# An RWKV block: a chunk's first columns set beside the product of k and v, the channel mix's gate through the hyperbolic tangent, and a new table of turns

## The chip, the cores and the metric

The kernel runs on one core of a Trainium2 chip. The engines of that core have short names in the profile: PE is TensorE (matmul; PEld is its weight load), DVE is VectorE, ACT is ScalarE, POOL is GpSimd and SP is SyncE, which here only issues transfers (DMA). The metric is device time in microseconds (us), the median of several runs; less is better.

## The reference, cut to what matters

The block takes x of shape 8 x 256 x 512 (batch, token, channel) in 32-bit floats and a state per batch. The 512 channels are 32 heads of 16.

```python
xn = _ln(x, ln1_w, ln1_b)
sx = _token_shift(xn, state[:, i1])                 # previous token minus this one
xxx = jnp.tanh((xn + sx * maa_x) @ maa_w1).reshape(b, l, 5, 1, EXTRA_MAA)
xxx = jnp.matmul(xxx, maa_w2).reshape(b, l, 5, E)
x5 = xn[:, :, None] + sx[:, :, None] * (maa_stack + xxx)
w = jnp.exp(-jnp.exp(time_decay + jnp.tanh(x5[:, :, 1] @ decay_w1) @ decay_w2))
r, k, v = x5[:, :, 3] @ Wr.T, x5[:, :, 0] @ Wk.T, x5[:, :, 2] @ Wv.T
g = jax.nn.silu(x5[:, :, 4] @ Wg.T)
def step(s, rkvw):                                  # one token after another
    a = k_t[:, :, :, None] * v_t[:, :, None, :]
    out = jnp.einsum('bhk,bhkd->bhd', r_t, u * a + s)
    return (a + w_t[:, :, :, None] * s, out)
...                                                 # att: group norm over the 16 values of a head
x = x + att * g @ Wo.T
xn2 = _ln(x, ln2_w, ln2_b)
sx2 = _token_shift(xn2, state[:, i0])
xk = xn2 + sx2 * ffn_maa_k
xr = xn2 + sx2 * ffn_maa_r
rr = jax.nn.sigmoid(xr @ ffn_Wr.T)                  # the gate of the channel mix
kk = jnp.square(jax.nn.relu(xk @ ffn_Wk.T))
x = x + rr * (kk @ ffn_Wv.T)
```

## The kernel before, in words

The code does not issue instructions as it goes along. A `Plan` first records each piece of work as an `Op` with its engine, the buffers that it writes and reads, and a function that issues it. Then `Plan.order` strings the pieces together as a list scheduler. It takes them by rank, lets a piece claim a buffer of a pool when one is free, and so fixes the order of the instructions on every engine and which buffer each piece gets. The rank comes from a table of numbers, `TURNS`, that has 25 rows: one for the setup, then for each of the eight batches one for `inputs_of_scan`, one for `scan` and one for `rest`. The planner's own costs of work and transfers (`LANDS`, `SWITCH` and others) decide where two pieces compete. After that each engine runs its list in order, and a piece waits on semaphores for what it needs.

`inputs_of_scan(b)` makes, for the 256 tokens of batch b, the layer norm (`xh`, `xn`), the token shift `sx`, the small product with a hyperbolic tangent (`psx`, `ta`), the five mixed inputs (`psm`, `mix`), the projections to k, v, r and g, and the decay w. `rest(b)` does the group norm, the output projection Wo, the second layer norm and the channel mix (Wfk, Wfr, Wfv), whose weights are streamed anew for each batch into buffers `Ws`. The helper `mul` (L401) issues the matmuls of all projections. Some of them are split into four of 32 columns.

`scan(b)` is the recurrence over tokens. It is split into 4 blocks of 4 chunks per batch, 128 chunks in all. A chunk holds 4 value columns of all heads: 128 partitions by 4 times 256 tokens. It passes these steps, with the line numbers before the change:

- A transfer by SP copies v, from memory, over the partitions into `vs` (128x1024). There are six buffers `vs`.
- L911, on ACT: the first column of each of the four stretches of 256 is overwritten with the state at the start (from `s0`, `cm`), 4 numbers per partition.
- L918, on DVE (6 of 128 chunks: L915, on POOL): the whole of `vs` is multiplied by k shifted by a token. The DVE reads k from a copy `kp` in PSUM, POOL reads the buffer of k itself. Column 0 of that k is set to one, so the first columns pass unchanged.
- L920, on DVE: the scan over the 1024 positions writes `st`, with `wrep` holding w, or zero at a stretch's first position. `wrep` is made by ACT in L901, once per block; there is one such buffer.
- L923, on POOL: `st` is multiplied by r.
- L931, on PE: after four chunks the gather of the block sums over the keys of a head into `pat`; L937, on DVE, adds it to `att`.

The channel mix has three gate lines: L1026 (ACT, Sigmoid from PSUM into `o`), L1051 and in the last batch L1044 (DVE, `o` times the product `psfv`). L1017 and L1018 (ACT) are Relu and Square of `kk`. ACT needs a table of functions for exp, tanh and the others. Where the next function is of another set, a table load (L1086) is put in front. Tanh was counted to the set of exp.

Other lines that are spoken of: L516 copies the centered weights Wv from PSUM (ACT), L534 makes four head masks `hm` (DVE), L613 transposes `xh`, L714 makes `ta` by Tanh (ACT), L743, L745 and L755 belong to the mixes of the first batch, L818 makes the decay (ACT), L856 the gate `g` by Silu, L997 and L1002 the group norm's end (`att` on ACT, `att` times `g` on POOL), L1008 adds x to the output projection (DVE).

Of the kernel before, what the change touches and what calls it, by code (L numbers as in the profile page):

```python
# [9 lines left out]
AF = mybir.ActivationFunctionType  # L10
ALU = mybir.AluOpType
# [47 lines left out]
class Op:  # L59
    def __init__(self, engine, us, outs, ins, emit, mode):  # L60
        self.engine, self.us, self.emit, self.mode, self.narrow = engine, us, emit, mode, False
        self.bufs = list(dict.fromkeys([*outs, *ins]))
        self.before, self.after, self.waits = [], [], 0
        self.ready = self.start = self.end = 0.0
        self.number, self.kind = 0, engine + "".join(c for c in self.bufs[0].name if not c.isdigit())


class Plan:
# [5 lines left out]
    LANDS = {"vs__": (2.3, 1.8), "rsb_": (0.9, 2.0), "sq_": (0.9, 2.0), "s": (0.2, 1.9), "vo_": (0.75, 2.2), "vo__": (0.38, 2.2), "o_": (0.75, 1.1), "x": (1.6, 1.7), "xt": (1.6, 1.7), "xs": (0.7, 0.9), "idt": (0.2, 2.2), "rd": (0.4, 1.4)}  # L74
    SWITCH = {"ACT": 1.3, "PE": 0.12}
    TABLES = {"exp": "exp_and_others", "silu": "silu_and_others", "sig": "sigmoid_and_others", "sqrt": "sqrt_and_others"}
# [15 lines left out]
    def add(self, engine, us, outs, ins, emit, mode=None, into=(), lag=0.0, kb=0, part=False):  # L92
# [3 lines left out]
        if kb:  # L96
            op.wire, op.lag = self.LANDS.get("".join(c for c in op.bufs[0].name if not c.isdigit()), (kb / 327, 2.3))

# [17 lines left out]
    def stage(self):  # L116
# [1045 lines left out]
```

## Time and profile before

| what | value |
| --- | --- |
| median of 3 runs | 609.05 us (608.36 to 609.75) |
| the profiled execution's own time | 609.75 us |
| its span in the profile | 607.9 us |
| granted TensorE clock | 1.00 throughout |
| PE busy | 598.3 us, 98% |
| DVE, ACT, POOL busy | 543.6, 514.6, 520.0 us |
| memory traffic | 124.76 MB, 205 GB/s on average |

The span runs from the first to the last instruction on the core. The time of the execution has 1.85 us more. PE is nearly always busy, but a share of busy time is an average: in the stretch from about 34 to 155 us POOL too is busy without a pause, and the last 28 us have hardly any work but matmuls. Weights and x are read in 512 KB transfers, the broadcasts of `vs` are 128 transfers of the same size.

### The profile page before, as it was taken

What the parts mean: (1) busy time and instruction counts of PE and PEld (TensorE: products, weight loads), DVE (VectorE), ACT (ScalarE), POOL (GpSimd) and SP (SyncE); (2) the same over time, 40 slices, a digit from 0 to 9 for tenths busy, and PEclk for the clock granted to TensorE, in tenths of its full rate; (3) what the DMA queues carried; (4) which work ended last, traced back from release to release, by engine and by line L of the source; (5) the groups of instructions that cost most, each with busy time, mean ns of one, the idle gap of its engine ahead of it and who ended that gap; (6) DMA issues with size and microseconds to landing.
All of it is one profiled execution on the core that took longest, in us unless ns stands there. A gap on an engine that the chain in (4) does not pass through costs nothing.

```text
span 607.9 us, 17606 instructions
## 1 busy us (share of the span) xinstructions
PE 598.3 (98%) x7270; PEld 346.1 (57%) x7270; DVE 543.6 (89%) x492; ACT 514.6 (85%) x1172; POOL 520.0 (86%) x417
## 2 busy tenths in 40 slices
PE   9999999999999999999999999999999999999997
PEld 7675555467544664377553775465644464547464
DVE  6699999999999998899889999999999999995442
ACT  5878779999999999998999898999989799966350
POOL 2899999999899999899988988999898998898020
PEclk9999999999999999999999999999999999999999
DMA  9889954878878887859677896788669877951552
GB/s 324 226 242 236 226 149 143 226 179 217 220 218 217 214 223 196 221 149 264 179 211 189 268 234 192 201 242 217 182 167 279 203 195 224 268 174 46 181 172 93
DMA packets 52639, 124.76 MB, mean 205 GB/s; under 512 B 5840, under 2 KB 11344, under 8 KB 52560
## 3 DMA queue, kind: packets, MB, share of 16 engines
q1 hardware_dynamic: 48048, 119.39, 71.4%
q10 hardware_dynamic: 4512, 4.26, 2.2%
q8 instruction: 57, 0.93, 0.7%
q14 instruction: 22, 0.18, 0.1%
HBM read 115.25 MB, written 8.39 MB: 203 GB/s over the span
## 4 chain that ended last, share of the span: by engine, by line
PE 72%; POOL 14%; ACT 4%; DVE 4%; issue 3%; DMA 1%; DVEq 0%; POOLq 0%; ACTq 0%
PE ps L401 59%; PE ps L931 7%; POOL st L923 7%; DVE st L920 2%; POOL mix L755 2%; PE ps L613 2%; POOL vs L915 2%; PE ps L795 2%; DMA vs<-vo 1%; ACT L1086 1%; PE ps L524 1%; POOL mix L783 1%; DVE vs L918 1%; POOL sx L641 1%; POOL att L887 1%
## 5 line engine op out<-in xcount | busy, mean ns | idle before, releaser
L920 DVE TENSOR_TENSOR_SCAN st<-wrep,vs 128x1024 f32<-128x1024 f32 x128 | 288.2, 2276 | 3.9 <-ACT wrep L901 1.8
L923 POOL TENSOR_TENSOR st<-st,r 128x1024 f32<-128x1024 f32 x128 | 254.5, 2006 | 9.4 <-DVE st L920 9.0
L918 DVE TENSOR_TENSOR vs<-vs,ps 128x1024 f32<-128x1024 f32 x122 | 143.7, 1207 | 4.2 <-ACT vs L911 4.0
L401 PE MATMUL ps<-Ws,mix 128*32 128x512 f32 (+3 forms) x872 | 115.8, 586 | 0.0
L401 PEld LDWEIGHTS ps<-Ws,mix 128*32 128x32 f32 (+1 forms) x872 | 38.4, 116 | 62.4 <-issue 55.6
L755 POOL TENSOR_TENSOR mix<-mix,xn 128x512 f32<-128x512 f32 x62 | 66.6, 1096 | 6.9 <-DVE mix L739 5.5
L931 PE MATMUL ps<-st,con 128*32 128x256 f32 x1024 | 62.1, 380 | 0.8 <-POOL st L923 0.7
L401 PE MATMUL ps<-mix,Wv 128*32 128x256 f32 (+1 forms) x832 | 60.5, 380 | 1.6 <-DVE mix L752 0.9
L401 PE MATMUL ps<-mix,Wk 128*32 128x256 f32 (+1 forms) x952 | 59.2, 379 | 0.1
L401 PE MATMUL ps<-mix,Wg 128*32 128x256 f32 (+1 forms) x664 | 58.8, 379 | 0.0
L401 PE MATMUL ps<-mix,Wr 128*32 128x256 f32 (+1 forms) x688 | 58.5, 380 | 0.0
L401 PE MATMUL ps<-mix,Ws 128*32 128x256 f32 (+1 forms) x664 | 57.7, 379 | 0.2 <-ACT mix L1017 0.2
L401 PE MATMUL ps<-Ws,g 128*32 128x512 f32 (+1 forms) x416 | 56.9, 593 | 0.2 <-POOL g L1002 0.2
L1086 ACT ACT_TABLE_LOAD x42 | 53.9, 1283 | 0.7
L737 ACT ACTIVATE ps<-ps,vec 128x256 f32<-128x256 f32 x112 | 47.6, 445 | 3.8 <-PE ps L401 2.3
L881 ACT COPY att<-ps 32x256 f32<-32x256 f32 x128 | 46.6, 364 | 4.4 <-ACT v L826 1.3
L669 POOL TENSOR_TENSOR mix<-mix,xn 128x512 f32<-128x512 f32 x44 | 47.3, 1093 | 3.4 <-ACT mix L667 3.3
L401 PEld LDWEIGHTS ps<-mix,Wv 128*32 128x32 f32 (+1 forms) x832 | 37.6, 116 | 21.3 <-DVE mix L752 1.6
L401 PEld LDWEIGHTS ps<-mix,Ws 128*32 128x32 f32 (+1 forms) x664 | 40.2, 124 | 15.8 <-ACT mix L1017 0.6
L401 PEld LDWEIGHTS ps<-mix,Wr 128*32 128x32 f32 (+1 forms) x688 | 39.3, 123 | 16.5 <-issue 1.3
L401 PEld LDWEIGHTS ps<-mix,Wg 128*32 128x32 f32 (+1 forms) x664 | 39.9, 124 | 14.8 <-issue 0.7
L931 PEld LDWEIGHTS ps<-st,con 128*32 128x32 f32 x1024 | 32.7, 110 | 27.5 <-issue 4.3
(134 smaller groups left out, 951.7 us busy)
## 6 DMA issues: line engine op xcount, KB each, us to landing
vs<-vo SPq DMA_DIRECT2D x128, 512.0 KB, 5.7
Ws<-in_fk SPq DMA_DIRECT2D x16, 512.0 KB, 5.8
Ws<-in_wo SPq DMA_DIRECT2D x16, 512.0 KB, 5.9
Ws<-in_fr SPq DMA_DIRECT2D x16, 512.0 KB, 6.1
Ws<-in_fv SPq DMA_DIRECT2D x16, 512.0 KB, 5.6
x<-in_x SPq DMA_DIRECT2D x9, 512.0 KB, 7.6
vo<-v ACTq DMA_DIRECT2D x15, 256.0 KB, 5.3
out<-o SPq DMA_DIRECT2D x15, 256.0 KB, 4.5
```

Source lines behind the costliest of these rows:

```text
L401: nc.tensor.matmul(out[i : i + n], lhsT=w[:, i : i + n], rhs=x, start=first, stop=final)
L613: nc.tensor.transpose(to[:, m, n * P : (n + 1) * P], xh[n]()[:, k * P : (k + 1) * P], idt())
L669: gp(512, t, [t, xn[q]], lambda q=q, t=t: nc.gpsimd.tensor_tensor(t(), t(), xn[q]()[:, :, 1 : T + 1], ALU.add))
L737: act(256, p_, [p_, vec], lambda g=g, q=q, m=m, p_=p_: nc.scalar.activation(p_()[:, m, :], p_()[:, m, :], AF.Identity, bias=col(f"maa_{g}" ...
L755: gp(512, t, [t, xn[q]], lambda q=q, t=t: nc.gpsimd.tensor_tensor(t(), t(), xn[q]()[:, :, 1 : T + 1], ALU.add))
L795: nc.tensor.matmul(pd()[i : i + 32, 0, :], lhsT=w, rhs=src[k // 2]()[:, k % 2, :], start=(k == begin), stop=(k == end))
L881: act(350, atts[q], [pc], lambda i=32 * (2 * q + m), m=m, q=q, h=32 * h: nc.scalar.copy(atts[q]()[h : h + 32, m, :], pc()[i : i + 32, 0, :]))
L918: dve(4 * T, [vs], [vs, kp], lambda m=m, vs=vs, kp=kp: nc.vector.tensor_tensor(vs(), vs(), kp()[:, m : m + 1, :].to_broadcast([P, 4, T]), ...
L920: dve(4 * T, [st], [w, vs], lambda w=w, vs=vs, st=st: nc.vector.tensor_tensor_scan(st().rearrange("p n t -> p (n t)"), w().rearrange("p n ...
L923: gp(4 * T, st, [st, r], lambda m=m, st=st, r=r: nc.gpsimd.tensor_tensor(st(), st(), r()[:, m : m + 1, :].to_broadcast([P, 4, T]), ALU.mul ...
L931: nc.tensor.matmul(pat()[32 * i : 32 * i + 32, 0, :], lhsT=con()[:, s : s + 32], rhs=done[i]()[:, j, :], start=(j == 0), stop=(j == 3),)
L1086: nc.scalar.preload_act_table_set(plan.TABLES[table])
```

## The change

Three edits in the code, and a new table.

**First columns.** The DMA of a chunk now writes `vs` under a second name, `landed`, and the ACT instruction that sets the first columns depends on `landed` and writes a third name, `first`. The product works on columns 1 to 255 of each stretch alone (128x4x255 in place of 128x1024), and only the scan needs `first`. So in the plan the product no longer follows the first columns. In the built program most of the DVE products waited on ACT before; now only some 15 of 122 do, and the scans wait on ACT.

**Gate.** Sigmoid becomes Tanh of half the argument, and the product becomes (`o` + 1) times `psfv` in one instruction with two operations. The missing factor of one half is put into Relu as a scale of 0.5**0.5 ahead of the Square. Tanh is counted to either the set of exp or that of silu, whichever is loaded. The program has 37 table loads with the one at its start, in place of 43. Up to the load for the square roots of batch 0's group norm it has 8 in place of 7.

**Turns and costs.** `TURNS` is another table, and some of the planner's costs are others. The number of pieces on each engine is unchanged: PE 400, DVE 490, ACT 1102, POOL 405, transfers 251. Of these PE has 185 in another place, mostly by one place and at most nine, DVE 341, ACT 968, POOL 293, transfers 211.

```diff
-    LANDS = {"vs__": (2.3, 1.8), "rsb_": (0.9, 2.0), ...}
+    LANDS = {"vs__": (2.3, 1.45), "rsb_": (0.5, 0.5), ...}
+    WAY = 1.4
+    TABLES = {"exp": "exp_and_others", "tanh": "exp_and_others", "silu": "silu_and_others", ...}
...
     TURNS = """
-        1 69 8 22 53 86 91 104 59 88 92 103 194 171 11 27 85 123 124 180 9 7 10 38 39 63 31 52 68 37 41 44 46 47 48,
+        8 74 18 43 53 81 61 64 90 79 102 99 173 150 5 33 118 145 151 146 24 15 34 26 47 49 31 46 56 30 35 48 32
...
+            if op.engine == "ACT":
+                if want == "tanh" and now in ("exp", "silu"):
+                    want = now
+                elif now == "tanh" and want in ("exp", "silu"):
+                    mode["ACT"] = now = want
...
-                    b.slot = max((s for s in self.pools[b.pool] if s[0] <= at), key=lambda s: s[0])
+                    b.slot = max((s for s in self.pools[b.pool] if s[0] + ahead <= at), key=lambda s: s[0])
...
+    def tables(self, ops):
+        mode = "sqrt"
+        for n, op in enumerate(ops):
+            want = op.mode
+            if want == "tanh":
+                want = mode if mode in ("exp", "silu") else next((o.mode for o in ops[n:] if o.mode != "tanh"), "exp")
+                want = "silu" if want == "silu" else "exp"
+            if want != mode:
+                op.table, mode = self.TABLES[want], want
...
+                landed, first = plan.fixed(vs, "landed"), plan.fixed(vs, f"vs{b}_{blk}_{i}")
...
-                act(4, vs, [s0, cm], lambda i=i, blk=blk, vs=vs: nc.scalar.activation(
+                plan.add("ACT", 0.19336, [first], [s0, cm, landed], lambda i=i, blk=blk, vs=vs: nc.scalar.activation(
                     vs()[:, :, 0:1], s0()[:, blk, 4 * i : 4 * i + 4].rearrange("p (n o) -> p n o", o=1),
-                    AF.Identity, bias=cm()[:, blk : blk + 1]), pointers=1)
+                    AF.Identity, bias=cm()[:, blk : blk + 1]), into=[vs])
...
-                        vs(), vs(), k.place[:, m : m + 1, 1 : T + 1].to_broadcast([P, 4, T]), ALU.mult), 1.815)
+                        vs()[:, :, 1:T], vs()[:, :, 1:T], k.place[:, m : m + 1, 2 : T + 1].to_broadcast([P, 4, T - 1]), ALU.mult), 1.95)
...
-                        vs(), vs(), kp()[:, m : m + 1, :].to_broadcast([P, 4, T]), ALU.mult))
-                dve(4 * T, [st], [w, vs], lambda w=w, vs=vs, st=st: nc.vector.tensor_tensor_scan(
+                        vs()[:, :, 1:T], vs()[:, :, 1:T], kp()[:, m : m + 1, 1:T].to_broadcast([P, 4, T - 1]), ALU.mult))
+                dve(4 * T, [st], [w, vs, first], lambda w=w, vs=vs, st=st: nc.vector.tensor_tensor_scan(
...
-            act(512, t, [ps], lambda t=t, ps=ps: nc.scalar.activation(t(), ps(), AF.Relu))
+            act(512, t, [ps], lambda t=t, ps=ps: nc.scalar.activation(t(), ps(), AF.Relu, scale=0.5**0.5))
...
-                o(), ps().rearrange("p m t -> p (m t)"), AF.Sigmoid), "sig")
+                o(), ps().rearrange("p m t -> p (m t)"), AF.Tanh, scale=0.5), "tanh")
...
-            dve(512, [o], [o, ps], lambda o=o, ps=ps: nc.vector.tensor_tensor(
-                o(), o(), ps().rearrange("p m t -> p (m t)"), ALU.mult))
+            dve(512, [o], [o, ps], lambda o=o, ps=ps: nc.vector.scalar_tensor_tensor(
+                o(), o(), 1.0, ps().rearrange("p m t -> p (m t)"), ALU.add, ALU.mult), 1.28)
```

What the table does is seen in the order of the instructions. Three places matter below. A row there reads line, operation, output<-inputs, shape and count; the number behind a name is the buffer's. Line numbers of the changed code are about 31 higher, so L401 is L432 there and L911 is L944.

The first place is the DVE at the head of the program, some 15 to 22 us into it: the mixes of the first batch (`mix`, L749, L752) and the head masks `hm`. Before:

```order
L749 SCALAR_TENSOR_TENSOR ps_172<-ps_172,vec,sx_104 128x256 x2
L752 TENSOR_TENSOR mix_115<-ps_172,xn_100 128x512
L534 TENSOR_SCALAR hm<-con,vec 128x32
L861 TENSOR_REDUCE cm_85<-s_83 128x4
L749 SCALAR_TENSOR_TENSOR mix_112<-ps_171,vec,sx_103 128x256
L749 SCALAR_TENSOR_TENSOR mix_114<-wrep_169,vec,sx_104 128x256 x2
L534 TENSOR_SCALAR hm<-con,vec 128x32 x2
L749 SCALAR_TENSOR_TENSOR mix_110<-ps_175,vec,sx_103 128x256 x2
```

And after the change, the same place:

```order
L780 SCALAR_TENSOR_TENSOR ps_175<-ps_175,vec,sx_104 128x256 x2
L783 TENSOR_TENSOR mix_115<-ps_175,xn_100 128x512
L780 SCALAR_TENSOR_TENSOR mix_110<-ps_172,vec,sx_103 128x256
L780 SCALAR_TENSOR_TENSOR mix_114<-wrep_169,vec,sx_104 128x256
L780 SCALAR_TENSOR_TENSOR mix_112<-ps_173,vec,sx_103 128x256
L780 SCALAR_TENSOR_TENSOR mix_114<-wrep_169,vec,sx_104 128x256
L780 SCALAR_TENSOR_TENSOR mix_110<-ps_172,vec,sx_103 128x256
L565 TENSOR_SCALAR hm<-con,vec 128x32
```

The masks have moved behind the products that POOL's next instructions read (`mix_114`, `mix_110`).

The second place is the same engine at the first chunks, some 28 to 36 us into the program. Before:

```order
L781 SCALAR_TENSOR_TENSOR mix_113<-ps_175,vec,sx_103 128x256
L918 TENSOR_TENSOR vs_145<-vs_145,ps_172 128x1024
L534 TENSOR_SCALAR hm<-con,vec 128x32
L920 SCALAR_TENSOR_TENSOR st_153<-wrep_169,vs_145 128x1024
L918 TENSOR_TENSOR vs_146<-vs_146,ps_172 128x1024
L920 SCALAR_TENSOR_TENSOR st_154<-wrep_169,vs_146 128x1024
```

After:

```order
L812 SCALAR_TENSOR_TENSOR mix_108<-ps_170,vec,sx_104 128x256
L951 TENSOR_TENSOR vs_145<-vs_145,ps_172 128x4x255
L953 SCALAR_TENSOR_TENSOR st_153<-wrep_169,vs_145 128x1024
L951 TENSOR_TENSOR vs_146<-vs_146,ps_172 128x4x255
L953 SCALAR_TENSOR_TENSOR st_154<-wrep_169,vs_146 128x1024
```

The last mask no longer stands between the first product and the first scan.

The third place is ACT at the decay and the gate of batch 1, some 80 to 93 us into the program, while batch 0 is in its scan's last blocks. `w` is the decay (L818), `g` the gate (L856), `vs` the first columns (L911). Before:

```order
L737 ACTIVATE ps_173<-ps_173,vec 128x256 x2
L1086 ACT_TABLE_LOAD
L856 ACTIVATE g_137<-ps_175 128x512
L1086 ACT_TABLE_LOAD
L818 ACTIVATE w_132<-ps_173,vec 128x256 x2
...
L826 COPY r_128<-ps_175 128x2x256
L1086 ACT_TABLE_LOAD
L856 ACTIVATE g_138<-ps_173 128x512
```

After:

```order
L1117 ACT_TABLE_LOAD
L887 ACTIVATE g_137<-ps_173 128x512
L944 ACTIVATE vs_148<-s_83,cm_85 128x4
L1117 ACT_TABLE_LOAD
L849 ACTIVATE w_132<-ps_174,vec 128x256
L944 ACTIVATE vs_147<-s_82,cm_84 128x4
L849 ACTIVATE w_133<-ps_172,vec 128x256
L849 ACTIVATE w_132<-ps_174,vec 128x256
L930 COPY ps_171<-k_125 128x512
L1117 ACT_TABLE_LOAD
L887 ACTIVATE g_138<-ps_173 128x512
L944 ACTIVATE vs_149<-s_83,cm_85 128x4
```

The second gate, `g_138`, now comes ahead of the last piece of the decay, and a further table load follows it. On PE the four matmuls of this decay stand ahead of batch 0's third gather; before they stood behind it.

More of the change, by code (lines that the diff above doesn't have):

```diff
@@ L61, in __init__ @@
         self.engine, self.us, self.emit, self.mode, self.narrow = engine, us, emit, mode, False
+        self.table = None
         self.bufs = list(dict.fromkeys([*outs, *ins]))
@@ L73 @@
     LATENCY = {"PE": 0.24, "DVE": 0.14, "ACT": 0.14, "POOL": 0.1, "DMA": 1.65}
-    LANDS = {"vs__": (2.3, 1.8), "rsb_": (0.9, 2.0), "sq_": (0.9, 2.0), "s": (0.2, 1.9), "vo_": (0.75, 2.2), "vo__": (0.38, 2.2), "o_": (0.75, 1.1), "x": (1.6, 1.7), "xt": (1.6, 1.7), "xs": (0.7, 0.9), "idt": (0.2, 2.2), "rd": (0.4, 1.4)}
+    LANDS = {"vs__": (2.3, 1.45), "rsb_": (0.5, 0.5), "sq_": (0.5, 0.5), "s": (0.3, 1.4), "vo_": (0.7, 1.4), "vo__": (0.35, 1.4),
+             "o_": (0.7, 1.2), "x": (1.8, 1.3), "xt": (1.7, 1.3), "xs": (0.7, 0.9), "idt": (0.2, 1.6)}
+    WAY = 1.4
+    TABLES = {"exp": "exp_and_others", "tanh": "exp_and_others", "silu": "silu_and_others", "sig": "sigmoid_and_others",
+              "sqrt": "sqrt_and_others"}
     SWITCH = {"ACT": 1.3, "PE": 0.12}
-    TABLES = {"exp": "exp_and_others", "silu": "silu_and_others", "sig": "sigmoid_and_others", "sqrt": "sqrt_and_others"}
     AHEAD = {"PE": 0.2}
@@ L96, in add @@
         if kb:
-            op.wire, op.lag = self.LANDS.get("".join(c for c in op.bufs[0].name if not c.isdigit()), (kb / 327, 2.3))
+            op.wire, op.lag = self.LANDS.get("".join(c for c in op.bufs[0].name if not c.isdigit()), (kb / 308, 1.7))
         op.bufs += [b for b in into if b not in op.bufs]
@@ L263, in order @@
         free = dict.fromkeys(self.LATENCY, 0.0)
-        mode, done, queue, put_off, wire, lanes = dict.fromkeys(free), [], [], [], 0.0, [0.0] * 8
+        mode, done, queue, put_off, wire, lanes = dict.fromkeys(free), [], [], [], [], [0.0] * 8
+        mode["ACT"] = "sqrt"
         for n, op in enumerate(self.ops):
@@ L303, in order @@
             if op.wire:
-                landed = max(wire if op.engine == "DMA" else 0.0, op.start + 1.2) + op.wire
-                wire = landed if op.engine == "DMA" else wire
+                landed = max([l for s, l in wire[-16:] if s <= op.start] + [op.start + self.WAY]) + op.wire
+                wire.append((op.start, landed))
                 lanes.append(landed + 1)
@@ L326, in order @@
         self.tiles([op for op in done if op.engine == "PE"])
+        self.tables([op for op in done if op.engine == "ACT" and op.mode])
         return done
+    def tables(self, ops):
[7 more added lines that the diff above has]
+                op.table, mode = self.TABLES[want], want
     def tiles(self, ops):
@@ L386, in new, with dma @@
         return Buf(pool, name, VIEWS.get(pool, lambda t: t))
-    def dma(out, in_, dst, kb, src=None, lag=0.0, part=False):
-        plan.add("DMA", 0.6, [out] if out else [], [src] if src else [], lambda: nc.sync.dma_start(out=dst(), in_=in_()),
+    def dma(out, in_, dst, kb, src=None, lag=0.0, part=False, also=()):
+        plan.add("DMA", 0.6, [out, *also] if out else [], [src] if src else [], lambda: nc.sync.dma_start(out=dst(), in_=in_()),
                  lag=lag, kb=kb, part=part)
@@ L533, in head_masks @@
         for k in range(NK):
-            dve(32, [hm], [con, vec], lambda k=k: nc.vector.tensor_scalar(
+            dve(76, [hm], [con, vec], lambda k=k: nc.vector.tensor_scalar(
                 hm()[:, k, :], con()[:, C_HM : C_HM + 32], col("faaaa", k), None, ALU.mult))
@@ L583, in normed @@
                     dve(512, [t], [s, mv, rs], lambda n=n, t=t, s=s: nc.vector.tensor_scalar(
[L584 removed]
+                        t(), s(), mv()[:, n, 0:1], rs()[:, n : n + 1], ALU.subtract, ALU.mult), 0.775)
                     xh.append(t)
@@ L627, in turned @@
                     dve(256, [xn], [ps, vec], lambda m=m, k=k, xn=xn, ps=ps: nc.vector.tensor_scalar(
-                        xn()[:, m, 1 : T + 1], ps()[:, m, :], col("ln1_w", k), col("ln1_b", k), ALU.mult, ALU.add))
+                        xn()[:, m, 1 : T + 1], ps()[:, m, :], col("ln1_w", k), col("ln1_b", k), ALU.mult, ALU.add), 1.5)
                     t = ps
@@ L633, in turned @@
                     dve(256, [xn], [ps, vec], lambda m=m, k=k, xn=xn, ps=ps: nc.vector.tensor_scalar(
-                        xn()[:, m, 1 : T + 1], ps()[:, m, :], col(f"ln{which}_w", k), col(f"ln{which}_b", k), ALU.mult, ALU.add))
+                        xn()[:, m, 1 : T + 1], ps()[:, m, :], col(f"ln{which}_w", k), col(f"ln{which}_b", k), ALU.mult, ALU.add), 1.5)
                 else:
@@ L713, in inputs_of_scan @@
             pe(0.432 * len(ks), [px], [w1, *dict.fromkeys(xin[k // 2] for k in ks)], mm, into=[ta])
-        act(256, ta, [px], lambda: nc.scalar.activation(ta(), px()[:, 0, :], AF.Tanh), "exp")
+        act(256, ta, [px], lambda: nc.scalar.activation(ta(), px()[:, 0, :], AF.Tanh), "tanh")
         def mixed():
@@ L800, in inputs_of_scan @@
         for rows in (slice(0, 64), slice(64, 128)):
-            act(T, hd, [pd], lambda rows=rows: nc.scalar.activation(hd()[rows, 1, :], pd()[0:64, 0, :], AF.Tanh), "exp")
+            act(345, hd, [pd], lambda rows=rows: nc.scalar.activation(hd()[rows, 1, :], pd()[0:64, 0, :], AF.Tanh), "tanh")
         for rows in (slice(0, 64), slice(64, 128)):
-            act(T, tb, [pd], lambda rows=rows: nc.scalar.activation(tb()[rows, :], pd()[64:128, 0, :], AF.Tanh), "exp")
+            act(345, tb, [pd], lambda rows=rows: nc.scalar.activation(tb()[rows, :], pd()[64:128, 0, :], AF.Tanh), "tanh")
         ws = [hd, new("w", f"w{b}_1")]
@@ L1043, in rest @@
                     pe(1.72 * wide / T, [ps], [*kk, *Wfv], mm, into=[y])
-                    dve(wide, [y], [o, ps], lambda yy=yy, o=o, ps=ps, cols=cols, wide=wide: nc.vector.tensor_tensor(
-                        yy()[:, cols], o()[:, cols], ps()[:, 0, 0:wide], ALU.mult))
+                    dve(wide, [y], [o, ps], lambda yy=yy, o=o, ps=ps, cols=cols, wide=wide: nc.vector.scalar_tensor_tensor(
+                        yy()[:, cols], o()[:, cols], 1.0, ps()[:, 0, 0:wide], ALU.add, ALU.mult), 1.28)
                     dve(wide, [y], [y, t], lambda yy=yy, t=t, cols=cols: nc.vector.tensor_tensor(
@@ L1079, in tile_rwkv_block @@
             phases[b + i].append((i, plan.stage()))
-    table = "sqrt"
     with tc.manual_schedule():
@@ L1083, in tile_rwkv_block @@
             narrow = op.narrow
-            if op.engine == "ACT" and op.mode and op.mode != table:
-                table = op.mode
-                nc.scalar.preload_act_table_set(plan.TABLES[table])
+            if op.table:
+                nc.scalar.preload_act_table_set(op.table)
             op.emit()
```

6 lines of the change are left out of this document (3 added, 3 removed), and 245 rows, old and new, of the table TURNS.

## The prediction

> **What bounds the kernel now.** I read the page first: the busy shares and the chain that ended last.
>
> ```profile
> PE 598.3 (98%) x7270; PEld 346.1 (57%) x7270; DVE 543.6 (89%) x492; ACT 514.6 (85%) x1172; POOL 520.0 (86%) x417
> PE 72%; POOL 14%; ACT 4%; DVE 4%; issue 3%; DMA 1%; DVEq 0%; POOLq 0%; ACTq 0%
> ```
>
> The change removes no matmul, so with PE at 598.3 us of a span of 607.9 all that can be won without making an instruction faster is PE's idle time, 9.6 us. Where that lies, and what fills it, a table of windows tells. Its columns are the window, its length, the busy time of PE, PEld, DVE, ACT and POOL with their instructions, the granted clock, the DMA share and GB/s.
>
> ```profile
> 0.00:34.30 34.30, 31.87 (x283) 24.81 (x284) 22.92 (x50) 25.73 (x61) 21.15 (x37) 1.00 0.82 260
> 34.30:155.40 121.10, 118.83 (x1734) 72.95 (x1731) 119.76 (x96) 105.70 (x246) 120.64 (x86) 1.00 0.79 206
> 155.40:312.00 156.60, 155.67 (x1969) 86.18 (x1968) 146.91 (x120) 148.32 (x343) 145.47 (x115) 1.00 0.77 208
> 312.00:580.00 268.00, 267.20 (x3207) 146.68 (x3200) 245.61 (x212) 226.26 (x510) 228.55 (x177) 1.00 0.74 206
> 580.00:608.00 28.00, 24.70 (x92) 15.45 (x89) 8.40 (x18) 8.62 (x15) 4.23 (x4) 1.00 0.34 113
> ```
>
> From 34.3 to 155.4 POOL has 120.64 us of work in 121.10. The list of its waits there has one line, and the timeline shows what ends the stretch: the multiplication by r of batch 1's last chunk (of its fourth block), and the gather that needs it.
>
> ```profile
> POOL st L923 <- DVE st L920: 0.2, 1, 0.2
> 153.33 2.02 POOL L923 TENSOR_TENSOR st<-st,r 128x1024 f32<-128x1024 f32 x1
> 155.49 1.93 PE L931 MATMUL ps<-st,con 128*32 128x256 f32 x32
> ```
>
> So POOL's work sets that this gather starts at 155.5. The 2.27 us in which PE is idle in this stretch are no gain by themselves: PE would reach the gather sooner and wait there. From 155.4 on PE is the bound, idle for 0.93 and 0.80 us in two windows, then 3.30 us in the last, most of it behind the last matmul. Its waits from 155.4 to the end are these:
>
> ```profile
> PE ps L401 <- DVE o L1051: 0.8, 1, 0.8
> PE ps L613 <- DVE xh L583: 0.4, 1, 0.4
> PE ps L401 <- ACT mix L1017: 0.2, 1, 0.2
> PE ps L401 <- DVE att L937: 0.2, 1, 0.2
> ```
>
> They add to 1.6 us. A gain has three places: POOL's start at 34.3, the length of POOL's stretch, and these waits.
>
> **First columns.** The groups that the chunk is made of (busy us and mean ns, then the idle time ahead of them and its releasers):
>
> ```profile
> L920 DVE TENSOR_TENSOR_SCAN st<-wrep,vs 128x1024 f32<-128x1024 f32 x128 | 288.2, 2276 | 3.9 <-ACT wrep L901 1.8 <-PE ps L931 0.9
> L918 DVE TENSOR_TENSOR vs<-vs,ps 128x1024 f32<-128x1024 f32 x122 | 143.7, 1207 | 4.2 <-ACT vs L911 4.0
> L911 ACT ACTIVATE vs<-s,cm 128x4 f32<-128x4 f32 x128 | 36.8, 299 | 4.5 <-DMA vs<-vo 3.3 <-ACT v L826 0.4
> L923 POOL TENSOR_TENSOR st<-st,r 128x1024 f32<-128x1024 f32 x128 | 254.5, 2006 | 9.4 <-DVE st L920 9.0
> ```
>
> The edit lets the product start without L911. What it can free is the 4.0 us that DVE waits for L911. The instruction of ACT stays (128 of 299 ns), and the scan, right behind the product on the same engine, waits for it instead. A product takes 1.2 us and a first column 0.3, so most of these waits are covered by the product from now on. But DVE is not the bound: the scan and the product make 1.207 + 2.276 = 3.48 us per chunk, yet in the stretch the end is set by POOL, which waited only 0.2 us for a scan, and after 155.4 by PE. Of the 4.0 us, 1.19 lie ahead of the very first product:
>
> ```profile
> 30.30 1.22 DVE L918 TENSOR_TENSOR vs<-vs,ps 128x1024 f32<-128x1024 f32 x1 [1.19 <-ACT vs L911]
> 31.44 0.58 DVE L534 TENSOR_SCALAR hm<-con,vec 128x32 f32<-128x32 f32 x1
> 31.94 2.28 DVE L920 TENSOR_TENSOR_SCAN st<-wrep,vs 128x1024 f32<-128x1024 f32 x1
> 34.30 2.00 POOL L923 TENSOR_TENSOR st<-st,r 128x1024 f32<-128x1024 f32 x1 [0.21 <-DVE st L920]
> 30.16 1.02 ACT L901 ACTIVATE wrep<-w 128x1020 f32<-128x1020 f32 x1
> ```
>
> There the scan also loses the mask between it and the product (0.50 us), and could start when `wrep` ends, at 31.18. POOL's wait began at 34.30 − 0.21 = 34.09; before that it was busy, so no more than the 0.21 us of its wait is won unless POOL's earlier work comes sooner.
>
> The product covers 1020 of 1024 elements: 4/1024 of 1207 ns is 5 ns, nothing. Its rows now start on the second word of each stretch. A row for such starts exists: the tile of L1008 is written from an odd word in one half of its instructions and from an even word in the other. The six products on POOL stand beside it.
>
> ```profile
> L1008 DVE TENSOR_TENSOR x<-ps,x x16: 667/684/694, 122.8 to 575.5; 128x512 f32<-128x512 f32 x16
> L915 POOL TENSOR_TENSOR vs<-vs,k x6: 2007/2202/2407, 40.2 to 123.9; 128x1024 f32<-128x1024 f32 x6
> ```
>
> L1008 spreads by 4% in all, and by no more between the halves, so I cost the odd start on DVE at nothing. On POOL three products take about 2.01 us and three about 2.4, by the block's place in k. The new addresses of k and `vs` differ, and which of the two prices the six take the trace can't say: 6 x (2.01 − 2.20) = −1.2 to 6 x (2.41 − 2.20) = +1.2 us, on the path, since POOL is without a pause. I take 0, the middle, and keep both ends.
>
> **The gate.**
>
> ```profile
> L1051 DVE TENSOR_TENSOR o<-o,ps 128x512 f32<-128x512 f32 x15 | 10.1, 678 | 17.6 <-PE ps L401 17.5
> L1044 DVE TENSOR_TENSOR o<-o,ps 128x256 f32<-128x256 f32 x1 | 0.4, 420 | 0.3 <-PE ps L401 0.3
> L662 DVE SCALAR_TENSOR_TENSOR mix<-sx,vec,xn 128x256 f32<-128x256 f32 x4 | 1.7, 478 | 0.0
> L1086 ACT ACT_TABLE_LOAD x42 | 53.9, 1283 | 0.7
> ```
>
> The instruction with two operations takes 478 − 420 = 58 ns more at 256 columns, so 0.06 to 0.12 at 512: under 2 us in 15 gates of DVE, off the path but for the last piece behind the last matmul, +0.1 at the end at most. Six loads fewer are 6 x 1.283 = 7.7 us of ACT. ACT is at 85%, and PE's waits for it after 155.4 are 0.2 us: worth nothing where they go.
>
> A rule speaks for more. The Trainium skill, page "ScalarE: Activation LUTs", section "What ACT_TABLE_LOAD costs", gives a switch 1283 ns and as much again, about 1380 ns, for a drain, 2.66 us in all; an estimate by it is 16 us of ACT for six. The trace agrees with the load alone:
>
> ```profile
> 11.42 1.28 ACT L1086 ACT_TABLE_LOAD   x1
> 12.71 0.38 ACT L714 ACTIVATE ta<-ps 128x256 f32<-128x256 f32 x1
> ```
>
> The next function starts 1.29 us after the load did, so 1.28 it is.
>
> **The turns: the head.** POOL's idle time in the mixes of batch 0, and the weights' product on PE that now goes ahead of `psx0`:
>
> ```profile
> 20.31 1.11 POOL L755 TENSOR_TENSOR mix<-mix,xn 128x512 f32<-128x512 f32 x1 [0.24 <-DVE mix L749]
> 22.32 2.15 POOL L755 TENSOR_TENSOR mix<-mix,xn 128x512 f32<-128x512 f32 x2 [0.90 <-DVE mix L749]
> 12.39 0.61 PE L401 MATMUL ps<-Ws,Ws 128*128 128x128 f32 x4
> ```
>
> The masks no longer stand ahead of the products that POOL waits for, so 0.24 + 0.90 = 1.14 us of POOL's idle time can go. Against it the 0.61 us of weights' products move ahead, and `ta` and all mixes come later by up to that. Together −0.5; but the copy of r now stands behind a first column and more on ACT, and the first multiplication by r needs `rk` and the scan. Late by one ACT piece (0.3) to two or three (1.0) is the other end: −0.5 to +1.0. I take +0.1, since the scan's own end (31.2 to 31.9, plus 2.28, so 33.5 to 34.2) is at the old time within that.
>
> **The turns: 34 to 155.** The same POOL work stands ahead of the last multiplication in both orders, so only new POOL waits count. ACT is the suspect: up to batch 0's square roots it has a load more.
>
> ```profile
> 82.19 1.28 ACT L1086 ACT_TABLE_LOAD   x1
> 85.33 0.84 ACT L818 ACTIVATE w<-ps,vec 128x256 f32<-128x256 f32 x2 [1.85 <-PE ps L401]
> 92.45 0.60 ACT L856 ACTIVATE g<-ps 128x512 f32<-128x512 f32 x1
> 114.70 1.09 ACT L997 ACTIVATE att<-att,vec 128x256 f32<-128x256 f32 x2
> 114.78 2.25 POOL L1002 TENSOR_TENSOR g<-att,g 128x512 f32<-128x512 f32 x2
> ```
>
> The load and the gate now ahead of the last decay are 1.28 + 0.60 = 1.88 us; the four decay matmuls moved ahead of the gather take away ACT's idle 1.85. These nearly cancel. The margin is thin: the second of the two L1002 starts about 114.78 + 2.25/2 = 115.9, and its input on ACT ends at 115.79. Any lateness of ACT over 0.1 us reaches POOL there. Between 0 and one load, 1.3: I take +0.2, near the end where the two cancel.
>
> **The turns: after 155.** Of the 1.6 us of PE's waits the largest (0.8) is a matmul that wants the PSUM buffer which a gate frees late; buffers and places are given anew, and that this very pair meets again is unlikely. I take 1.2 of 1.6 as gone. New waits of the same kind may come: nothing to 3 us, the old sum twice; I take +0.3, because the planner now keeps a margin for a buffer on PE.
>
> The sum: +0.1 + 0 + 0.2 − 1.2 + 0.3 + 0.1 = −0.5, from the profiled execution's 609.75 to 609.25. That execution is 0.70 above the median of the runs, 609.05, so the forecast is 608.5. Less than 0.2%, 1.2 us here (607.8 to 610.3), can hardly be told from no change.
>
> **The rivals.**
>
> - Faster: all PE waits after 155 go and no new ones come (−1.6), and the POOL products all take the short price (−1.2), with POOL's head half a microsecond sooner (−0.5) or not. 609.05 − 2.8 = 606.2, to 605.7. For it: each term has its row. Against it: the products' price is a toss, and a new order brings waits of its own.
> - Slower: ACT's added load reaches POOL. Place: the decay of batch 1 and the pair L997 and L1002 at 115. It decides from the point where `att` is ready more than 0.1 us later than POOL is, and from there each microsecond goes to the gather at 155.5 and the end, since POOL has no pause that could take it up. Price: 1.88 us if the idle 1.85 is not regained, 1.88 + 1.28 if a load falls at 115 too; in place of 0.2 this gives 608.5 + 1.7 = 610.2, to 611.5. Against it: the decay's matmuls do move ahead.
> - The product is slower from an odd word. As a mechanism of this kernel: POOL's product differs by 2407/2007, 20%, with the address alone; the same on DVE is 0.24 us for each product. The products of the stretch to 155, by the windows for L918 alone:
>
> ```profile
> 34.30:155.40 121.10, 32.83 (x28) 1.00 0.79 206
> ```
>
> 28 x 0.24 = 6.7 us, of which DVE's idle time there, 121.10 − 119.76 = 1.3, can take up 1.3; the end moves by 5.4 us, from 608.5 to about 614, and more if the products behind 155 bind too. Against it: L1008 does not differ between its halves. The Trainium skill, page "Vector Engine (DVE) Microarchitecture Reference", passage "The SBUF access granule: adjacent pairs", states such a rule: full rate only for runs that start on an 8-byte boundary, 1.30 against 1.054 ns a column for pairs from an odd word; L1008 here does not bear it out.
> - The edit of the first columns frees nothing, because the scan waits for L911 in place of the product: the 4.0 us stand at L920 then. As DVE is not the bound the time is the same, 608.5 to 609; it counts with the forecast.
>
> **How the numbers follow.** The forecast has 0.48 (its own range 607.3 to 610.0), the faster rival 0.27, the slower 0.18, the odd start 0.05; 0.02 is left for a stall that I don't see. Faster by over 0.2%: 0.27 and 0.07 of the forecast, 0.34. Slower: 0.15 of the second rival, 0.04 of the forecast, 0.05 and 0.02, 0.26. The rest, 0.40, is no change. The range goes from 605.7, the faster rival's end, to 611.4, the slower one's.
>
> **What would show it.** In the profile after: the waits of L918 for ACT are gone and L920 has some; ACT has 36 loads; the gate's rows are at 0.74 to 0.80 us; L918 stays at about 1.2 us. POOL is without a pause from about 34.4 until the gather of batch 1's last block, near 155.7. PE's waits after that are about 0.7 us. The forecast is wrong if POOL shows waits over 1 us between 35 and 155, if the six POOL products all take 2.0 or all 2.4, or if PE's waits after 155 are over 2 us.

## The result, and the profile after

The changed kernel takes 615.62 us (median of 4 runs, 614.28 to 617.54), the kernel before 609.26 on the same chip (608.36 to 609.75). The ratio is 1.0106, with a 95% interval from 1.0087 to 1.0126: slower by 6.4 us. The forecast was 608.5, in a range from 605.7 to 611.4. The profiled execution is the slowest of the four (617.54, span 615.8); its runs also scatter more than those of before, 3.3 against 1.4 us.

The page's busy shares and chain, after:

```profile
PE 599.6 (97%) x7246; PEld 349.9 (57%) x7246; DVE 543.5 (88%) x492; ACT 508.5 (83%) x1166; POOL 520.1 (84%) x417
PE 56%; POOL 15%; ACT 14%; DVE 5%; DMA 5%; issue 4%; ACTq 0%; DVEq 0%; POOLq 0%
```

Nobody has more work: DVE 543.5 against 543.6 us, POOL 520.1 against 520.0, ACT 6 less. In the chain PE has lost 16 points, and DMA has 5% where it had 1%. The windows, cut at the same events as before (the join of batch 1's last gather is now at 157.6):

```profile
0.00:34.30 34.30, 31.35 (x277) 23.97 (x278) 22.33 (x49) 25.94 (x62) 20.64 (x36) 1.00 0.84 264
34.30:157.60 123.30, 118.47 (x1740) 74.13 (x1739) 119.00 (x96) 107.47 (x248) 120.62 (x86) 1.00 0.80 207
157.60:312.00 154.40, 152.36 (x1781) 86.17 (x1784) 144.42 (x118) 140.99 (x330) 143.35 (x115) 1.00 0.74 199
312.00:580.00 268.00, 266.52 (x3350) 147.28 (x3342) 243.69 (x205) 224.98 (x511) 230.81 (x179) 1.00 0.74 206
580.00:616.00 36.00, 30.91 (x109) 18.32 (x107) 14.03 (x27) 9.10 (x18) 4.62 (x4) 0.98 0.33 115
```

POOL's stretch has the same 120.6 us of work but is 2.2 us longer. Behind it PE is idle for 2.04 and 1.48 us where it was for 0.93 and 0.80. The waits name two things. First, DVE's and POOL's waits for the transfer of `vs`. Before had no such row for these two engines: there the products waited 4.0 us for first columns on ACT, and those 3.3 us for transfers. Then PE's waits from 157.6 on, 4.2 us in all:

```profile
DVE vs L951 <- DMA vs<-vo: 7.8, 6, 2.3
POOL vs L948 <- DMA vs<-vo: 2.3, 1, 2.3
```

```profile
PE ps L432 <- ACT w L849: 1.7, 1, 1.7
PE ps L432 <- DVE mix L693: 1.4, 1, 1.4
PE ps L432 <- POOL att L1026: 0.4, 1, 0.4
PE ps L432 <- POOL mix L700: 0.3, 2, 0.2
PE ps L432 <- ACT o L1059: 0.2, 1, 0.2
PE ps L432 <- DVE o L1084: 0.2, 1, 0.2
```

**Transfers that land late.** The chain goes through three transfers of `vs`:

```profile
51.88 10.55 DMA vs<-vo
281.41 10.40 DMA vs<-vo
361.52 11.43 DMA vs<-vo
```

The median of all `vs` from issue to landing is 5.8 us, and it was 5.7 before; these three take 10.4 to 11.4. A long transfer alone is nothing new: before had eight that took over 9 us, the longest 13.3, but there the product stood at least 2.6 us behind the landing. What stands ahead of the first is seen in SP's timeline, and what it holds up in POOL's. That timeline's columns are the start, the time taken, engine, line, operation and count.

```profile
49.22 1.16 SPq L421 DMA_DIRECT2D vs<-vo  x2
50.43 0.84 SPq L421 DMA_DIRECT2D x<-in_x  x1
51.32 0.46 SPq L421 DMA_DIRECT2D xt<-in_x  x1
51.88 3.07 SPq L421 DMA_DIRECT2D vs<-vo  x2
62.56 1.99 POOL L948 TENSOR_TENSOR vs<-vs,k 128x1020 f32<-128x1020 f32 x1 [2.27 <-DMA vs<-vo]
```

Two transfers of x, 512 KB each, are issued between the first pair of `vs` and the second. Before, SP issued the four `vs` of this block without anything between them:

```profile
49.96 6.37 SPq L390 DMA_DIRECT2D vs<-vo  x4
```

POOL, which has no pause in this stretch, waits 2.27 us for the product's input, and the join comes about as much later (157.6 against 155.5). At 281 and 361 us it is DVE that waits.

**Two engines at once, in the tail.** DVE's four mixes of the last batch (L693, before L662) are twice as long as before while POOL runs its additions (L700), and PE waits for them. The first row is before, the others after:

```profile
582.26 1.67 DVE L662 SCALAR_TENSOR_TENSOR mix<-sx,vec,xn 128x256 f32<-128x256 f32 x4
```

```profile
588.53 3.34 DVE L693 SCALAR_TENSOR_TENSOR mix<-sx,vec,xn 128x256 f32<-128x256 f32 x4
589.09 2.50 POOL L700 TENSOR_TENSOR mix<-mix,xn 128x512 f32<-128x512 f32 x2 [22.76 <-DVE mix L693]
591.93 5.45 PE L432 MATMUL ps<-mix,Ws 128*128 128x256 f32 x24 [1.44 <-DVE mix L693]
```

**The edits themselves** cost what the groups say:

```profile
L951 DVE TENSOR_TENSOR vs<-vs,ps 128x1020 f32<-128x1020 f32 x122 | 143.0, 1203 | 8.4 <-DMA vs<-vo 7.8 <-ACT ps L930 0.6
L953 DVE TENSOR_TENSOR_SCAN st<-wrep,vs 128x1024 f32<-128x1024 f32 x128 | 288.9, 2278 | 4.6 <-PE ps L964 1.1 <-ACT vs L944 0.7 <-POOL mix L700 0.6
L948 POOL TENSOR_TENSOR vs<-vs,k x6: 1993/2206/2403, 40.6 to 121.5; 128x1020 f32<-128x1020 f32 x6
L1084 DVE SCALAR_TENSOR_TENSOR o<-o,ps 128x512 f32<-128x512 f32 x15 | 10.1, 681 | 16.7 <-PE ps L432 16.7
L1117 ACT ACT_TABLE_LOAD x36 | 46.2, 1283 | 0.6
34.72 2.00 POOL L956 TENSOR_TENSOR st<-st,r 128x1024 f32<-128x1024 f32 x1
```

The product from an odd word takes 1203 ns for 1207; the gate 681 for 678; POOL's products keep their two prices; the scan waits 0.7 us for first columns in all. POOL's first multiplication by r (last row) starts 0.4 us later than before. So the edits are not where the time went, unless by what they let move.

### The profile page after: what moved, and what is told of

Its sections match the earlier page's. It is cut to its first block, busy times and chain, and to the rows that moved or that the text cites. A ratio compares the mean times of both kernels' runs of the same rounds, so it can differ in the third digit from the quotient of the medians.

```text
span 615.8 us, 17481 instructions
## 1 busy us (share of the span) xinstructions
PE 599.6 (97%) x7246; PEld 349.9 (57%) x7246; DVE 543.5 (88%) x492; ACT 508.5 (83%) x1166; POOL 520.1 (84%) x417
## 4 chain that ended last, share of the span: by engine, by line
PE 56%; POOL 15%; ACT 14%; DVE 5%; DMA 5%; issue 4%; ACTq 0%; DVEq 0%; POOLq 0%
PE ps L432 46%; POOL st L956 8%; DMA vs<-vo 5%; PE ps L964 5%; POOL mix L786 2%; PE ps L644 2%; PE ps L826 2%; POOL mix L700 2%; ACT L1117 1%; DVE st L953 1%; ACT mix L698 1%; ACT sq L1023 1%; ACT ps L768 1%; ACT wrep L932 1%; PE ps L555 1%
## 5 line engine op out<-in xcount | busy, mean ns | idle before, releaser
L951 DVE TENSOR_TENSOR vs<-vs,ps 128x1020 f32<-128x1020 f32 x122 | 143.0, 1203 | 8.4 <-DMA vs<-vo 7.8
L432 PE MATMUL ps<-Ws,mix 128*32 128x512 f32 (+3 forms) x872 | 115.7, 586 | 0.4 <-DVE o L1084 0.2
L432 PEld LDWEIGHTS ps<-Ws,mix 128*32 128x32 f32 (+1 forms) x872 | 38.4, 116 | 62.7 <-issue 52.1
L700 POOL TENSOR_TENSOR mix<-mix,xn 128x512 f32<-128x512 f32 x44 | 47.7, 1099 | 29.1 <-DVE mix L693 22.8
L786 POOL TENSOR_TENSOR mix<-mix,xn 128x512 f32<-128x512 f32 x62 | 66.9, 1098 | 6.1 <-DVE mix L770 5.8
L432 PE MATMUL ps<-mix,Wv 128*32 128x256 f32 (+1 forms) x856 | 59.8, 379 | 1.5 <-DVE mix L783 1.0
L432 PE MATMUL ps<-mix,Wg 128*32 128x256 f32 (+1 forms) x664 | 58.6, 380 | 2.6 <-ACT w L849 1.7
L432 PE MATMUL ps<-mix,Wr 128*32 128x256 f32 (+1 forms) x832 | 59.2, 380 | 0.0
L432 PE MATMUL ps<-mix,Wk 128*32 128x256 f32 (+1 forms) x760 | 59.0, 379 | 0.0
L432 PE MATMUL ps<-mix,Ws 128*32 128x256 f32 (+1 forms) x664 | 57.5, 379 | 1.4 <-DVE mix L693 1.4
L432 PE MATMUL ps<-Ws,g 128*32 128x512 f32 (+1 forms) x416 | 57.1, 593 | 1.5 <-POOL g L1035 1.5
L432 PEld LDWEIGHTS ps<-mix,Wg 128*32 128x32 f32 (+1 forms) x664 | 40.5, 124 | 17.6 <-issue 2.5
L432 PEld LDWEIGHTS ps<-mix,Ws 128*32 128x32 f32 (+1 forms) x664 | 40.0, 124 | 17.2 <-DVE mix L693 1.8
L432 PEld LDWEIGHTS ps<-mix,Wv 128*32 128x32 f32 (+1 forms) x856 | 38.6, 115 | 18.7 <-DVE mix L783 1.4
L432 PEld LDWEIGHTS ps<-mix,Wk 128*32 128x32 f32 (+1 forms) x760 | 39.3, 119 | 17.4 <-issue 1.5
L432 PEld LDWEIGHTS ps<-mix,Wr 128*32 128x32 f32 (+1 forms) x832 | 36.7, 116 | 19.5 <-issue 2.0
```

The lines of the kernel that those rows point to most:

```text
L432: nc.tensor.matmul(out[i : i + n], lhsT=w[:, i : i + n], rhs=x, start=first, stop=final)
L700: gp(512, t, [t, xn[q]], lambda q=q, t=t: nc.gpsimd.tensor_tensor(t(), t(), xn[q]()[:, :, 1 : T + 1], ALU.add))
L786: gp(512, t, [t, xn[q]], lambda q=q, t=t: nc.gpsimd.tensor_tensor(t(), t(), xn[q]()[:, :, 1 : T + 1], ALU.add))
L951: dve(4 * T, [vs], [vs, kp], lambda m=m, vs=vs, kp=kp: nc.vector.tensor_tensor(vs()[:, :, 1:T], vs()[:, :, 1:T], kp()[:, m : m + 1, 1:T].t ...
```

## The experiments

The theories: A, the new turns lose the time, through late transfers of `vs`; C, the tail loses some through DVE and POOL beside each other; B, the edits lose it. Times are medians, and ratios are to the kernel before on the same chip.

**Both edits in the old order.** The table of turns fixes the order of all engines, as far as what each piece needs allows it; the planner's costs then only choose buffers. So the edits can be run in exactly the order of before:

```diff
-    TURNS = """ (new)          LANDS, WAY and the other costs (new)
+    TURNS = """ (of before)    LANDS, WAY and the other costs (of before)
```

> Both edits (first columns, gate) with the turns and the planner's costs of before. Theory A (the new turns lose the time, by standing products where their transfers land late and by a collision of DVE and POOL in the tail; the edits themselves are about neutral): 609.3 us as before, between 607.5 and 610.5, and DVE's waits for a transfer of vs under 2 us. Theory B (the edits lose it: without the first column ahead of it the product stands too early and the scan waits instead): 613 to 616, with scans that wait for ACT.

Measured: 608.53 us, ratio 0.9994 (0.9985 to 1.0002). Theory B falls: the edits cost nothing in the old order, and win nothing that can be measured. No product waits for a transfer. The matmul records and POOL's work are as many as before, and ACT has 8.8 us less, with seven loads fewer:

```profile
PE 597.1 (98%) x7270; PEld 343.9 (57%) x7270; DVE 543.1 (90%) x492; ACT 505.8 (83%) x1165; POOL 520.0 (86%) x417
```

**The new order without the edits.** The code of before with the new `TURNS` and costs:

> The code of before with the new table of turns and the new costs, without the two edits. Theory A: slow like the changed kernel, 614 to 618, with late transfers of vs ahead of the first columns or products. Theory B: 608 to 610.5.

Measured: 683.27 us, ratio 1.1213 (1.1179 to 1.1248), far beyond what both theories said. DVE's waits show most of it:

```profile
DVE vs L929 <- ACT vs L922: 51.3, 27, 7.6
```

In the changed kernel 56 of the 128 first columns start later than the product that they once stood ahead of. Where the product needs them again, it is put later: 114 of DVE's 490 pieces and 14 of POOL's 405 stand elsewhere than in the changed kernel, while ACT, PE and the transfers keep its order. The granted clock was lower too, 0.965 in this run, and PE was busy for 620.2 us in place of 599.6, so part of the loss may lie in longer matmuls. Two more runs separated the edits within the new order. In the first the gate is as before (Sigmoid, the plain product) and the first columns are changed:

> The changed kernel with Sigmoid and the plain product for the gate, in exactly the changed kernel's order, which gives 48 table loads behind the first in place of 36. Theory A (the 67 us of the run with the turns alone were the first columns ahead of the product): 616 to 622, up to the 12 more loads' 15 us of ACT where ACT is late. Rival E (the new order cannot bear the loads of Sigmoid): 660 or more.

Measured: 630.36 us, ratio 1.035 (1.0334 to 1.0365): outside both expectations. There are 49 loads in the list, the order of every engine is the changed kernel's, and what waits for ACT now is PE:

```profile
L1117 ACT ACT_TABLE_LOAD x49 | 62.9, 1283 | 0.8
PE ps L432 <- ACT o L1059: 8.7, 5, 5.2
```

The 13 loads more are 16.7 us of ACT, and 14.7 us of time is lost. PE's waits for the gate on ACT are 8.7 us of it; that the loads cost the rest too is likely, since little else differs, but it is not shown. In the second the gate goes through Tanh and the product waits for the first columns again:

> The changed kernel with the first columns ahead of the product again, so that the product waits for ACT, and the gate through Tanh. The ACT, PE and SP orders are the changed kernel's. Theory A: 665 to 685, with DVE's waits for the first columns near 50 us. Rival E: 616 to 622.

Measured: 671.08 us, ratio 1.1011 (1.0985 to 1.1037), as theory A said. DVE and POOL have the order of the run with the turns alone:

```profile
DVE vs L949 <- ACT vs L942: 43.1, 26, 5.7
```

So in the new order the edit of the first columns is worth 55 us (671.08 − 615.62), with the pieces of DVE and POOL that stand elsewhere and a lower granted clock (0.987 in the profiled execution, PE busy for 610.5 us) counted in, and that of the gate 15. In the old order both together are worth nothing measurable.

**The old order with new buffers.** Both edits, the old `TURNS`, the new costs:

> Both edits with the old table and the new costs of the planner. The order of every engine is that of before; the costs only give pieces other buffers. Theory A (the order alone carries the loss): 607.5 to 610. Rival D (the new choice of buffers makes pieces wait for each other): 612 or more.

Measured: 608.63 us, ratio 0.9999 (0.9991 to 1.0008). In the old order the choice of buffers doesn't matter; the order carries the loss.

**Transfers put back, first attempt.** In the changed kernel nine transfers are issued later on SP. Nothing is changed on the other engines:

```diff
-        for op in plan.order(phases):
+        ops = plan.order(phases)
+        behind("DMA", ["x20", "xt3"], "vs0_2_1")                         # behind: right after that piece
+        behind("DMA", ["vs4_1_0", "Wfk2_1", "o1_1", "Wfr2_0"], "vs4_0_2")
+        behind("DMA", ["vs5_1_2", "x25", "xt7"], "vs5_0_3")
+        for op in ops:
```

> The changed kernel with its order kept on every engine but SP: at three places (52, 281 and 361 us) the transfers of x, of weights and of an output that are issued just ahead of a late vs are issued behind it. Theory A: the three waits of 2.3, 3.2 and 1.4 us for vs go, and 3 to 4.5 us of the 6.4 come back: 611.0 to 612.5. Rival A2 (the transfers are late because of the whole traffic, not of the ones right ahead; or what is moved back is late in its turn): 614.5 to 616.5.

Measured: 613.43 us, ratio 1.0076 (1.006 to 1.0093): 1.8 us of 6.4 by the ratios, half of what was expected and between the two forecasts. The reason lies in the attempt: at two places it put a `vs` back too, and that one came late instead.

```profile
293.13 2.34 DVE L951 TENSOR_TENSOR vs<-vs,ps 128x1020 f32<-128x1020 f32 x2 [1.84 <-DMA vs<-vo]
368.16 1.22 DVE L951 TENSOR_TENSOR vs<-vs,ps 128x1020 f32<-128x1020 f32 x1 [2.90 <-DMA vs<-vo]
```

**The tail's order.** In the changed kernel POOL's last four additions are put in the order of before:

```diff
+        behind("POOL", ["xr7_1"], "o6_1")
+        behind("POOL", ["xr7_0"], "o6_0")
```

> The changed kernel with POOL's last four additions in the order of before: o6 of a half ahead of xr7, so that POOL starts after DVE's four mixes at 588.5 us. Theory C (the four mixes took 3.34 in place of 1.67 us because POOL ran its additions beside them): they take 1.67 us again, PE's wait of 1.44 us for them goes, and the time falls by 1.4 us to 614.2 (613.5 to 615). Rival (something else in the new order makes them long): still 3.3 us and no gain, 615.6.

Measured: 613.75 us, ratio 1.0076 (1.0062 to 1.009), 1.8 us less. The four mixes of DVE are back at their old length, although nothing on DVE was touched:

```profile
588.14 1.67 DVE L693 SCALAR_TENSOR_TENSOR mix<-sx,vec,xn 128x256 f32<-128x256 f32 x4
```

**Both repairs.** The tail as above, and eleven transfers behind the late `vs` at four places, no `vs` among them:

```diff
+        behind("DMA", ["x20", "xt3"], "vs0_2_1")
+        behind("DMA", ["Wfk2_1", "o1_1", "Wfr2_0"], "vs4_0_2")
+        behind("DMA", ["o2_0", "o2_1", "x25", "xt7"], "vs5_0_3")
+        behind("DMA", ["Wo5_0", "Wo6_1"], "vs6_3_0")
```

> The changed kernel with both repairs: POOL's tail as in the run on the tail, and at four places (52, 281, 361 and 461 us) transfers of x, weights or outputs issued behind the vs that was late, without putting another vs back as the first attempt did at 281 and 361. Theory A with C: the two gains add and the third place is now won too: 610.0 to 611.5, with waits of products for vs under 3 us in all. Rival A2 (transfers put back are late in their turn, and one place's gain is the next one's loss): 612.5 to 614.

Measured: 609.04 us, ratio 1.0004 (0.9996 to 1.0013), better than expected: the whole loss is gone. SP now issues the four `vs` together, POOL's product starts 2.5 us sooner and waits for nothing, and DVE waits for one `vs`:

```profile
49.07 5.67 SPq L421 DMA_DIRECT2D vs<-vo  x4
54.79 0.58 SPq L421 DMA_DIRECT2D x<-in_x  x1
60.03 2.02 POOL L948 TENSOR_TENSOR vs<-vs,k 128x1020 f32<-128x1020 f32 x1
DVE vs L951 <- DMA vs<-vo: 1.5, 1, 1.5
```

PE's waits behind the join (from 156 us on) are down to these:

```profile
PE ps L432 <- POOL mix L700: 0.2, 1, 0.2
PE ps L432 <- DVE o L1084: 0.2, 1, 0.2
```

**The transfers alone.** The same eleven, without the tail:

> The repaired kernel without the repair of the tail: eleven transfers of x, weights and outputs stand behind the late vs at four places, POOL's order is the changed kernel's. If the two causes are separate and add (theory A with C): the four mixes of DVE take 3.3 us again and the time is 1.5 to 1.9 us above the repaired kernel's 609.0: 610.5 to 611.2. Rival (the tail's cost depends on what happened before it, or the transfers account for all): within 0.6 us of 609.0, or above 612.

Measured: 610.76 us, ratio 1.0031 (1.002 to 1.0043). No product waits for a transfer any more, and the tail's waits are back:

```profile
L693 DVE SCALAR_TENSOR_TENSOR mix<-sx,vec,xn x4: 480/894/1318, 581.7 to 583.7; 128x256 f32<-128x256 f32 x4
PE ps L432 <- DVE mix L693: 1.4, 1, 1.4
```

The four ratios make a square. The transfers are worth 1.0106 − 1.0031 = 0.75% with the bad tail and 1.0076 − 1.0004 = 0.72% with the good one, 4.4 to 4.6 us. The tail is worth 0.30% and 0.27%, 1.6 to 1.8 us. Together they are 1.02%, 6.2 us of the 6.4; the 0.04% that is left lies within the repaired kernel's interval.

**Can both kernels be beaten?** The gathers of the repaired kernel stood about 1 us behind those of before up to 260 us, and most of them level or ahead from 310 on. So the old order was taken for the first part and the repaired new one for the rest, with the seam at 199 us and at 252 us:

```diff
-                op.rank = int(t)
+                op.rank = t if t < SPLICE else SPLICE + u    # t of the old table, u of the new; SPLICE 925, then 1169
```

> Both edits; the order of before for its first 925 pieces of work (up to 199 us), then that of the new table, with the three later groups of transfers put behind the late vs and the tail's POOL order, as in the repaired kernel. In the repaired kernel the gathers stood 1.25 us behind before at 194 us and 0.14 us ahead of it from 316 on; with the old order the edits stood 0.5 us ahead at 194. If the stretches add (theory A): 607.2 us (606.5 to 608.0), faster than before by 0.2 to 0.4%. Rival F (what one stretch wins is only what it lost before, or the seam costs more): 608.5 or more.

> The same with the seam at piece 1169 (252 us), behind PE's wait of 0.8 us for a gate at 250 us: theory A 607.4 to 608.2, a little more than with the earlier seam; rival F 608.5 or more.

Measured: 608.58 us, ratio 0.9995 (0.9985 to 1.0005), and 609.33, ratio 1.0005 (0.9994 to 1.0017). Rival F holds: nothing that can be told from before. Every order without late transfers and without the collision in the tail ends within 0.1% of before.

## Why the prediction was wrong

- **The step that failed first is "The turns: 34 to 155"**: "so only new POOL waits count. ACT is the suspect". POOL's new wait was for a transfer, 2.27 us, and ACT held POOL up there for 0.2 us at most. With it the prediction's own sign of being wrong came, a wait of POOL over 1 us between 35 and 155. The text on the change said that 211 of 251 transfers stand in another place; the prediction priced none of them, had no rival for them and never looked at SP. What should have been read is, for each chunk, when its transfer is issued and lands and where its product stands in the new order. The time from landing to product in the trace of before is not enough: it is 3 to 10 us for 80 of the 128 chunks, and for the seven chunks that came late it was 4.7 and 7.7 us at 52 us, 13.5, 19.7 and 0.4 at 281, 5.1 at 361 and 3.5 at 461. The table moved both ends. POOL's product at the first place started at 66.9 us before and starts at 60.0 in the repaired kernel, and its transfer took 10.55 us behind the two of x but 7.85 with these issued later. At 361 the transfer took 11.43 us, and 5.18 with four others issued later.
- **"New waits of the same kind may come: nothing to 3 us, the old sum twice; I take +0.3"** was the second: the waits at 281 and 361 us are of another kind, again for transfers. PE's waits behind the join became 4.2 us, over the 2 us that the prediction named as its other sign of being wrong. With the place at 52 us the missing term measures 4.4 to 4.6 us.
- **The gate's tail, "+0.1 at the end at most"**, looked only at the gate's own instruction. The new order of POOL's last additions let two engines meet; no term stood for that, and it measures 1.6 to 1.8 us.
- **What held.** The odd start on DVE costs nothing (1203 ns), the POOL products nothing (2.20 us in the mean both times), and 36 loads are there. POOL's first multiplication by r starts at 34.7 in place of 34.3, inside −0.5 to +1.0. The waits of PE behind the join fall to 0.4 us in the repaired kernel from 1.6, as "1.2 of 1.6" had it. The repaired kernel's 609.04 is 0.5 us from the forecast of 608.5, so the rest of the sum was small, as forecast; the half microsecond that it was to win is not there. By the profiled executions the gather at the join starts 0.8 us later than before (156.31 for 155.49) where the sum had +0.3, and the stretch behind it is 0.6 us shorter where the sum had −0.8.
- **What was wrong in size only.** The gate was expected at 0.74 to 0.80 us and has 681 ns: the row that priced it (478 against 420) compared an instruction with all its inputs in SBUF with one that reads PSUM. With one input in PSUM both take the same: 422 ns after and 420 before for the last batch's piece of 128x256.
- **The rivals.** The slower one had the right sign by the wrong mechanism: ACT's added load did not reach POOL. The rule on odd starts would have given 614, near the measured time, and is refuted by its own row; a time that agrees proves no mechanism.

What stays open: why the table brings transfers and products so close. The changed costs price transfers anew, but in the programs run here they only choose buffers, and how the table was made no run can show.

## What to carry to other kernels

Where a change moves the issue of transfers, take for each consumer the time between landing and use in the old trace, and ask how far the new order moves the use and the issue, and which moved transfer now stands ahead on the same queue: the order of one queue was worth 0.7% here with every byte and every engine's work unchanged. Price an edit in the order in which it will run: the same two edits were worth nothing measurable in one order and some 55 and 15 us in the other. When the order of two engines changes near the end, look for instructions of DVE with two inputs in SBUF that meet POOL's reads of SBUF.

## What the runs showed of the hardware

Of the four mixes of DVE in the tail, which have both inputs in SBUF, two take 480 ns in the changed kernel as they do alone; the two that meet an addition of POOL take 1317 and 1307 ns, and the two additions 1273 and 1213 ns in place of 1090. The Trainium skill, page "SBUF — State Buffer", section "SBUF: two separate sides", has the rule: a DVE instruction with two SBUF inputs and a GpSimd instruction that reads SBUF take a shared pair of ports in turn, and the second waits for the whole of the first. The trace agrees: each long mix ends 0.28 us after the addition beside it (at 590.64 and 591.87 us, the additions at 590.36 and 591.59). The first row below is the run with the tail's order of before; the others are the changed kernel, where the numbers behind the count are the least, the median and the most in ns. The last row has the products, which have one input in PSUM and run beside POOL all along without being longer:

```profile
L693 DVE SCALAR_TENSOR_TENSOR mix<-sx,vec,xn x4: 479/479/480, 588.1 to 589.3; 128x256 f32<-128x256 f32 x4
```

```profile
L693 DVE SCALAR_TENSOR_TENSOR mix<-sx,vec,xn x4: 480/894/1317, 588.5 to 590.6; 128x256 f32<-128x256 f32 x4
590.56 1.31 DVE L693 SCALAR_TENSOR_TENSOR mix<-sx,vec,xn 128x256 f32<-128x256 f32 x1
L951 DVE TENSOR_TENSOR vs<-vs,ps x122: 1157/1206/1218, 29.9 to 552.1; 128x1020 f32<-128x1020 f32 x122
```
